# Involutions of a four-layer network: 7x7 as band-matrix products on TensorE, 3x3 summed by identity matmuls

## Chip, cores and metric

One core of a Trainium2 chip runs the whole network. The metric is the device time of one execution in microseconds. Everything is computed in float32.

## What is computed

The input is 16 images of 64 x 64 tokens with 256 channels. Four layers follow each other, each as `x = x + layer(group_norm(x))`: linear attention (layer 0), a gated layer with a selective scan and a batch norm over all images (layer 1), a 3x3 involution (layer 2) and a 7x7 involution (layer 3). The change concerns the end of layer 1 and layers 2 and 3.

```python
def _L2_conv_ref(x, Wr, br, gamma, beta, mean, var, Ws, bs, Wi, bi):
    r = einsum('bhwc,cd->bhwd', x, Wr) + br
    r = relu((r - mean) * rsqrt(var + 1e-3) * gamma + beta)
    w = einsum('bhwd,dk->bhwk', r, Ws) + bs
    w = w.reshape(B, H, W, 16, 9)[:, :, :, :, None, :]
    xi = einsum('bhwc,cf->bhwf', x, Wi) + bi
    patches = stack of the 9 shifted copies of the zero-padded xi
    patches = patches.reshape(B, H, W, 16, 16, 9)
    return sum(w * patches, axis=-1).reshape(B, H, W, 256)

def _L3_conv_ref(x, w_reduce, gamma, beta, mean, var, w_span, b_span):
    r = einsum('bhwc,cd->bhwd', x, w_reduce)
    r = relu((r - mean) * (gamma / sqrt(var + 1e-3)) + beta)
    kgen = (einsum('bhwd,de->bhwe', r, w_span) + b_span).reshape(B, H, W, 16, 49)
    patches = stack of the 49 shifted copies of the zero-padded x
    return einsum('bhwgk,bhwkgc->bhwgc', kgen, patches).reshape(B, H, W, 256)
```

An involution is a convolution whose weights are made at each token from the token itself: 64 reduced features give 9 or 49 weights for each of 16 groups of 16 channels. In layer 2 the patch array is reshaped as it lies in memory: the flat index `q = tap * 256 + channel` is cut into runs of nine, so that an output channel sums nine neighbours of the flat index, which are mostly nine channels of one tap.

## The kernel before

The program has two halves. The first (up to L531) runs layer 0 and most of layer 1 for one image after the other, stores the result channel by channel in the DRAM tile `x1_d`, and collects the statistics of the batch norm. The second half (from L534) runs over the 16 images again. What follows is one image of it.

**End of layer 1 (L613 to L638).** In eight chunks of 512 tokens `x1` is loaded from `x1_d` (L617); the token factors are spread over the partitions by four matmuls (`pf`, L123); ScalarE applies scale and shift (L622), VectorE multiplies by `pf` (L626), ScalarE applies the relu (L627), GpSimd adds `x1` and writes `xl` (L631), VectorE takes the statistics (L637). `xl` holds 128 channels on the partitions and two halves; a token of row 32 g + r, column w lies at (r, w, g), so two rows make a line of 128 tokens.

**Layer 2 projections (L641 to L663).** Each chunk is normalised into `xn` by ScalarE and VectorE (L105, L106). TensorE makes the 64 reduced features (`pr`, L649) and the projection `xi` (`px`, L658). ScalarE writes them to `rt` (L652) and to the padded planes `pad` (L662). GpSimd copies the halo between the two halves (L596, L597).

**3x3 involution (L667 to L710).** Eight groups of four lines. For each of three column shifts TensorE transposes six lines of `pad` (L604) and ScalarE copies them to `xs` (L677), so that 128 tokens lie on the partitions. TensorE makes the weights `pw` in PSUM (L682). VectorE multiplies segment by segment into `pd` (L691, 40 instructions per group, sorted by column shift), sums nine neighbours with one reduction (L698) and adds the residual, which TensorE has transposed into `pres` (L705, L710). The result is `x3`.

**Layer 3 norm and reduction (L713 to L741).** `x3` is transposed back (L718), copied into `pad` (L723), its statistics taken (L727); `pad` is normalised in place (L105, L106), the reduced features are made (L734, L738), and the halo is copied again.

**7x7 involution (L744 to L805).** Four blocks of eight lines; in each, seven column shifts `dj`. Per shift TensorE transposes 14 lines into `xs` (L604, copied out by ScalarE in L756). Per half block of four lines TensorE makes the weights `pk` (L761), VectorE multiplies seven row shifts (L770), GpSimd adds pairs of products (L782), and TensorE sums the four remaining terms in PSUM by multiplying them with the identity (`pacc`, L787). After the seventh shift VectorE adds `x3` (L797) and SyncE stores the rows (L801).

All DMAs are issued on SyncE's queue (SP). The program is written in a framework that puts the instructions of each engine into one order ahead of the run, from data dependences and free buffers; each engine then runs its own list in order and waits on semaphores. Buffers of a pool are reused in turn, and a pool that is closed gives its memory to the next one.

Of the kernel before, what the change touches and what calls it, by code (L numbers as in the profile page):

```python
# [15 lines left out]
P = 128  # L16
# [10 lines left out]
PAD = 3  # L27
PW = HW + 2 * PAD
PR = HW // 2 + 2 * PAD


def involution_segments():
    """The flat patch index q = tap * 256 + channel, cut where the tap, the group (q // 144) or
    a run of nine changes: (tap, first channel, q, groups of nine, elements in each)."""
    cuts = sorted(set(range(0, 2305, 256)) | set(range(0, 2305, 144)))
    out = []
    for a, b in zip(cuts, cuts[1:]):
        head = min(b, -(-a // 9) * 9)
        tail = max(head, b // 9 * 9)
        for lo, hi, n in ((a, head, head - a), (head, tail, 9), (tail, b, b - tail)):  # L40
            if hi > lo:
                out.append((lo // 256, lo % 256, lo, (hi - lo) // n, n))
    # One column shift after the other.
    return sorted(out, key=lambda s: s[0] % 3)
# [3 lines left out]
def network(ctx: ExitStack, tc: tile.TileContext, a: dict, out: bass.AP):  # L48
# [19 lines left out]
    # Kept for all images: gate and normalisation of layer 1 (scale, shift), and its token factor.  # L68
    ab = const("ab", [P, 2, NI, 2])
    fac = const("fac", [P, NI, NB])  # L70
    bnp = const("bnp", [P, 2, 2])
    x1_d = dram.tile([NI, 2, P, NT], F32, tag="x1_d", name="x1_d")

    def inv_sqrt(dst, var, eps):
        """dst = (var + eps) ** -0.5 of a narrow tile"""
        n = dst.shape[-1]
        v = small.tile([P, n], F32, tag=f"isq{n}", name="isq")
        nc.vector.tensor_scalar(v, var, eps, None, ALU.add)  # L78
        nc.gpsimd.tensor_tensor(dst, v, mhalf[:, :n], ALU.pow)  # L79

    def group_norm(stats, pool):
        """Mean and 1/std of each channel's group, [128, 2] each, from its bn_stats."""
# [20 lines left out]
    def normalised(dst, src, gm, rstd, nb):  # L103
        """dst = (src - mean) * rstd over [128, 2, n]: a channel half on each engine."""
# [5 lines left out]
    def affine(dst, src, i):  # L110
        """Layer 1's gated input of image i over [128, 2, n]."""
# [7 lines left out]
    def spread(pf, i, ch):  # L119
        """Token factors of a chunk on every partition."""  # L120
# [10 lines left out]
    # ------------------------------------------------------------------ layers 0 and 1  # L131
    with ExitStack() as st:
# [20 lines left out]
        # Rows of the scan's inputs: delta, delta m m, delta m, m, 1.  # L153
# [10 lines left out]
        # The 7x7 convolution as matrices between the tokens of two row pairs, delta pairs apart.  # L164
# [40 lines left out]
        for i in range(NI):  # L205
            # x, channels on partitions
# [19 lines left out]
            # linear attention, four heads at a time: tokens t = 128 d + p, channels 8 j + head  # L226
            oa = []
            for hf in range(2):
# [32 lines left out]
                # k: softmax over (p, j) for each (d, head); its sum comes with the context  # L261
# [19 lines left out]
                # q: softmax over d for each (p, j, head); its sum divides the product  # L281
# [51 lines left out]
            # output projection, layer norm, residual; statistics for layer 1  # L333
# [57 lines left out]
            # layer 1: channel gate  # L391
# [27 lines left out]
            nc.vector.tensor_scalar(ab[:, 1, i, :], gate, -1.0, None, ALU.mult)  # L419

            # mean and maximum over channels, [p, d] with two zero columns on each side
# [18 lines left out]
            # selective scan: softplus, then the inputs of the recurrence as rows  # L440
# [61 lines left out]
            # statistics of the gated product for the batch norm over all images  # L502
# [13 lines left out]
        # Over images of one size: the mean of their means; of their variances, and the means' own.  # L516
# [21 lines left out]
    # ------------------------------------------------------------------ layers 1 (end), 2, 3  # L538
    with ExitStack() as st:
# [3 lines left out]
        tr = st.enter_context(tc.tile_pool(name="b_tr", bufs=2, space=PSUM))  # L543
# [15 lines left out]
        wsp = bconst("wsp", [65, 7, 112])  # L559
        wspf = wsp.rearrange("p j k -> p (j k)")  # L560
        nc.sync.dma_start(out=wspf[0:64, :], in_=a["w_span"])
        nc.sync.dma_start(out=wspf[64:65, :], in_=a["b_span"])

        def folded(name, mean, var, gamma, beta, shift):
            """(v + shift - mean) * gamma / sqrt(var + eps) + beta as scale and bias, [64, 2]"""
# [6 lines left out]
            sb = bconst(f"{name}_sb", [64, 2])  # L572
# [5 lines left out]
            nc.vector.tensor_tensor(sb[:, 1:2], v[:, 0:1], v[:, 3:4], ALU.add)  # L578
            return sb
# [4 lines left out]
        # From here on a token of row 32 g + r, column w is (r, w, g): two rows are 128 tokens in a  # L584
        # line. The padded planes hold both halves with their halo; what lies outside stays zero.
        pad = big.tile([P, 2, PR, PW, 2], F32, tag="pad", name="pad")
        nc.gpsimd.memset(pad, 0.0)
        # Reduced features, with a row of ones for the bias.
        rt = big.tile([65, NT], F32, tag="rt", name="rt")
        nc.gpsimd.memset(rt[64:65, :], 1.0)  # L590
        lines = pad.rearrange("p c e w g -> p c e (w g)")
        inner = lines[:, :, PAD : PAD + 32, 2 * PAD : 2 * (PAD + HW)]

        def halo():
            cols = pad[:, :, :, PAD : PAD + HW, :]
            nc.gpsimd.tensor_copy(cols[:, :, 0:3, :, 1], cols[:, :, 32:35, :, 0])  # L596
            nc.gpsimd.tensor_copy(cols[:, :, 35:38, :, 0], cols[:, :, 3:6, :, 1])  # L597

        segments = involution_segments()

        def shifted(dst, line, col):
            """The 128 tokens of a line, seen from a shift: dst [128, 256] in PSUM."""
            for h in range(2):
                nc.tensor.transpose(  # L604
                    dst[:, h * P : (h + 1) * P], lines[:, h, line, 2 * col : 2 * col + P], ident
                )

        for i in range(NI):
            xl = big.tile([P, 2, NT], F32, tag="xl", name="xl")
            x3 = big.tile([P, 32, C], F32, tag="x3", name="x3")  # L610
            st0 = wk.tile([P, 2, NCH, 6], F32, tag="st0", name="st0")
            with ExitStack() as ph:
                w1 = ph.enter_context(tc.tile_pool(name="b_w1", bufs=2))  # L613
                for ch in range(NCH):
                    tk = slice(ch * CT, (ch + 1) * CT)
                    x1 = w1.tile([P, 2, CT], F32, tag="x1", name="x1", bufs=3)
                    nc.sync.dma_start(out=x1, in_=x1_d[i, :, :, tk].rearrange("h p t -> p h t"))  # L617
                    pf = sm.tile([P, CT], F32, tag="sm", name="pf")
                    spread(pf, i, ch)
                    for h in range(2):  # L620
                        z = w1.tile([P, CT], F32, tag="z", name="z", bufs=3)
                        nc.scalar.activation(  # L622
                            z, x1[:, h], AF.Identity,
                            bias=ab[:, 1, i, h : h + 1], scale=ab[:, 0, i, h : h + 1],
                        )
                        nc.vector.tensor_tensor(z, z, pf, ALU.mult)  # L626
                        nc.scalar.activation(z, z, AF.Relu, bias=bnp[:, 1, h : h + 1])  # L627
                        dst = xl[:, h].rearrange("p (r w g) -> p g r w", r=32, g=2)[
                            :, ch // 4, ch % 4 * 8 : ch % 4 * 8 + 8, :
                        ]  # L630
                        nc.gpsimd.tensor_tensor(  # L631
                            dst,
                            z.rearrange("p (r w) -> p r w", w=HW),
                            x1[:, h].rearrange("p (r w) -> p r w", w=HW),
                            ALU.add,
                        )
                        nc.vector.bn_stats(st0[:, h, ch, :], dst)  # L637
            _, gm, rstd, nb = group_norm(st0, sm)  # L638

            with ExitStack() as ph:  # L640
                w2 = ph.enter_context(tc.tile_pool(name="b_w2", bufs=2))  # L641
                mm = ph.enter_context(tc.tile_pool(name="b_mm", bufs=2, space=PSUM))
                for ch in range(NCH):
                    tk = slice(ch * CT, (ch + 1) * CT)
                    xn = w2.tile([P, 2, CT], F32, tag="t", name="xn")
                    normalised(xn, xl[:, :, tk], gm, rstd, nb)
                    pr = sm.tile([P, CT], F32, tag="sm", name="pr")
                    for h in range(2):
                        nc.tensor.matmul(  # L649
                            pr[0:64, :], lhsT=wr2[:, h, :], rhs=xn[:, h], start=(h == 0), stop=(h == 1)  # L650
                        )
                    nc.scalar.activation(  # L652
                        rt[0:64, tk], pr[0:64, :], AF.Relu, bias=sb2[:, 1:2], scale=sb2[:, 0:1]
                    )
                    for fh in range(2):
                        px = tr.tile([P, CT], F32, tag="tr", name="px")
                        for h in range(2):
                            nc.tensor.matmul(  # L658
                                px, lhsT=wi[:, h, fh * P : (fh + 1) * P], rhs=xn[:, h],
# [5 lines left out]
                            AF.Identity, bias=bi[:, fh : fh + 1],  # L665
                        )
                halo()  # L667
# [209 lines left out]
```

## Time and profile before

| | us |
|---|---|
| median of 3 runs (21,822.43 to 21,828.05) | 21,826.8 |
| span of the profiled execution | 21,826.7 |
| TensorE matmul busy | 16,690.8 |
| TensorE weight loads busy | 10,255.7 |
| VectorE busy | 14,419.2 |
| GpSimd busy | 7,388.4 |
| ScalarE busy | 5,343.7 |

Busy times are sums over one execution. Weight loads (PEld) run beside matmuls (PE). A line of a table of groups names the source line, the engine and the operation, then output and inputs, the shapes, the number of instructions, the busy time and the mean duration of one, and at the end the idle time of the engine ahead of them with what ended it. In the table by stage each engine has its busy time and, in brackets, its number of instructions; "PEclk" is the granted clock of TensorE as a share of full speed. In a timeline a line has the start, the length and what ran. Matmuls are pipelined: the durations of neighbours overlap, and the cost of one in a row is the distance of two starts.

### The profile page before, as it was taken

Reading aid. Unit: us, or ns where it says so; the run is one execution under the profiler, and the core shown is the slowest. Engines: PE = TensorE matmul, PEld = TensorE weight load, DVE = VectorE, ACT = ScalarE, POOL = GpSimd, SP = SyncE. Lnnn points to the kernel's source line nnn. Section 1 sums busy time; section 2 is a strip of 40 time slices with the busy share of each in tenths; the row PEclk is TensorE's granted clock in tenths of the full one; section 3 lists DMA queues with packets and bytes.
Section 4 is the critical chain, followed back from the end, with each engine's and each line's share of the span. In section 5 each row is a group of like instructions: output and inputs, shape, how many; then the busy total and the mean of one; then the engine's idle time right before and its main releaser. Section 6 shows DMA issues by size and latency. Waiting matters only on the chain.

```text
span 21826.7 us, 175959 instructions
## 1 busy us (share of the span) xinstructions
PE 16690.8 (76%) x66336; PEld 10255.7 (47%) x66336; DVE 14419.2 (66%) x19055; ACT 5343.7 (24%) x8944; POOL 7388.4 (34%) x3593
## 2 busy tenths in 40 slices
PE   6776666666666669779788797797887977878779
PEld 4444444444444434445444454454444544544445
DVE  4444444444444467878778777777787777877878
ACT  2222222222222222222222222222222222222221
POOL 0000110000001016436355363363543634635436
PEclk7777776677777669889889898898987988989889
DMA  0000000000000000000000000000000000000000
GB/s 29 16 16 16 21 19 16 16 24 16 16 18 21 17 6 16 4 12 6 12 14 4 12 16 2 14 6 12 14 4 12 15 3 14 6 10 16 4 12 8
DMA packets 212129, 282.07 MB, mean 13 GB/s; under 512 B 13116, under 2 KB 145421, under 8 KB 211278
## 3 DMA queue, kind: packets, MB, share of 16 engines
q1 hardware_dynamic: 211278, 270.81, 3.7%
q8 instruction: 523, 8.57, 0.2%
q14 instruction: 328, 2.69, 0.0%
HBM read 136.55 MB, written 134.22 MB: 12 GB/s over the span
## 4 chain that ended last, share of the span: by engine, by line
PE 41%; DVE 18%; POOL 4%; issue 3%; ACT 1%; DMA 1%; SPq 0%; DVEq 0%; POOLq 0%; ACTq 0%
PE pacc L787 28%; DVE pd L691 7%; DVE lo L698 6%; PE pt L604 4%; POOL prod L782 3%; PE pk L761 3%; DVE prod L770 2%; PE px L658 2%; PE pr L649 1%; PE pr L734 1%; POOL xl L631 1%; DVE st L727 0%; DVE ot L797 0%; PE pt L718 0%; ACT z L627 0%
## 5 line engine op out<-in xcount | busy, mean ns | idle before, releaser
L770 DVE TENSOR_TENSOR prod<-xs,pk 128x1024 f32<-128x1024 f32 x6272 | 7152.2, 1214 | 1675.0 <-PE pk L761 1405.9
L782 POOL TENSOR_TENSOR prod<-prod 128x1024 f32<-128x1024 f32 x2688 | 6279.3, 2365 | 2612.8 <-DVE prod L770 2594.3
L787 PE MATMUL pacc<-prod,ident 128*128 128x512 f32 x14336 | 6652.3, 598 | 304.5 <-POOL prod L782 304.4
L787 PEld LDWEIGHTS pacc<-prod,ident 128*128 128x128 f32 x14336 | 2528.4, 191 | 2632.0 <-issue 2226.5
L756 ACT COPY xs<-pt 128x512 f32<-128x512 f32 x3136 | 1753.1, 588 | 6852.6 <-PE pt L604 6449.8
L604 PE MATMUL pt<-ident,pad 128*128 128x128 f32 x17152 | 2730.3, 300 | 518.1 <-ACT xs L677 411.9
L604 PEld LDWEIGHTS pt<-ident,pad 128*128 128x128 f32 x17152 | 2183.3, 154 | 1682.3 <-issue 832.9
L691 DVE TENSOR_TENSOR pd<-xs,pw 128x576 f32<-128x576 f32 (+16 forms) x5120 | 1569.5, 386 | 222.2 <-ACT xs L677 222.2
L241 PE MATMUL pq<-wq,xn 128*128 128x384 f32 x4096 | 1398.6, 505 | 135.3 <-DVE va L257 92.3
L79 POOL TENSOR_TENSOR gn_r<-isq,mhalf 128x2 f32<-128x2 f32 x64 | 44.9, 701 | 4227.2 <-DVE isq L78 4227.2
L698 DVE TENSOR_REDUCE lo<-pd 128x1024 f32<-128x9216 f32 x128 | 1247.6, 9747 | 3.3
L761 PEld LDWEIGHTS pk<-wsp,rt 65*128 65x128 f32 x7168 | 959.0, 192 | 417.9 <-issue 417.9
L241 PEld LDWEIGHTS pq<-wq,xn 128*128 128x128 f32 x4096 | 807.5, 198 | 709.2 <-issue 161.4
L677 ACT COPY xs<-pt 128x512 f32<-128x512 f32 x1152 | 634.9, 588 | 1818.0 <-DVE pd L691 1493.3
L761 PE MATMUL pk<-wsp,rt 65*128 65x112 f32 x7168 | 970.2, 272 | 0.0
L286 POOL TENSOR_TENSOR qa<-qa,mq 128x2048 f32<-128x2048 f32 x64 | 231.7, 3642 | 1841.7 <-DVE mq L283 1841.7
L123 PE MATMUL pf<-ident,fac 128*128 128x128 f32 x2048 | 443.1, 388 | 429.4 <-DVE z L626 323.9
L705 PE MATMUL pres<-ident,xl 128*128 128x128 f32 x1024 | 244.9, 408 | 678.4 <-DVE x L710 678.3
L375 PE MATMUL pt<-ident,y 128*128 128x128 f32 x1024 | 268.4, 436 | 638.1 <-DVE y L368 638.1
L423 POOL MEMSET maps<- 128x72 f32 x16 | 2.5, 158 | 1940.1 <-PE psc L491 1940.1
L257 DVE COPY va<-pq 128x256 f32<-128x256 f32 x512 | 215.9, 424 | 661.5 <-ACT ka L253 636.4
L473 DVE TENSOR_TENSOR_SCAN hst<-da,hst,pbc 16x512 f32<-16x512 f32 x112 | 142.0, 1268 | 770.1 <-PE pbc L469 770.1
(186 smaller groups left out, 17910.2 us busy)
## 6 DMA issues: line engine op xcount, KB each, us to landing
xin<-in_x SPq DMA_DIRECT2D x128, 512.0 KB, 4.5
x_d<-xT SPq DMA_DIRECT2D x128, 512.0 KB, 2.8
x<-x_d SPq DMA_DIRECT2D x128, 512.0 KB, 3.6
out<-ot SPq DMA_DIRECT2D x256, 256.0 KB, 2.8
wq<-in_wqkv SPq DMA_DIRECT2D x1, 768.0 KB, 5.0
wo<-in_wout SPq DMA_DIRECT2D x1, 256.0 KB
wi<-in_Wi SPq DMA_DIRECT2D x1, 256.0 KB
bmask<-in_bmask SPq DMA_DIRECT2D x1, 224.0 KB, 2.6
```

Source lines behind the costliest of these rows:

```text
L123: nc.tensor.matmul(pf[:, q * P : (q + 1) * P], lhsT=fac[:, i, d : d + 1].broadcast_to([P, P]), rhs=ident, start=True, stop=True,)
L241: nc.tensor.matmul(pq[:, dd, 0:384], lhsT=xn[:, h, tok], rhs=wq[:, h, hf * 384 : (hf + 1) * 384], start=(h == 0), stop=(h == 1),)
L604: nc.tensor.transpose(dst[:, h * P : (h + 1) * P], lines[:, h, line, 2 * col : 2 * col + P], ident)
L658: nc.tensor.matmul(px, lhsT=wi[:, h, fh * P : (fh + 1) * P], rhs=xn[:, h], start=(h == 0), stop=(h == 1),)
L677: nc.scalar.copy(t[:, e : e + 2, :], pt)
L691: nc.vector.tensor_tensor(pd[:, :, q0 : q0 + n].rearrange("p r (f k) -> p r f k", k=nk), xs[dj][:, di : di + 4, c0 : c0 + n].rearrange("p ...
L698: nc.vector.tensor_reduce(lo, pd.rearrange("p r (o k) -> p r o k", k=9), AX.X, ALU.add)
L756: nc.scalar.copy(xs[:, e : e + 2, :], pt)
L761: nc.tensor.matmul(pk[:, r, 0:112], lhsT=rt[:, row * P : (row + 1) * P], rhs=wsp[:, dj, :], start=True, stop=True,)
L770: nc.vector.tensor_tensor(t.rearrange("p r (g c) -> p r g c", c=16), xs[:, g * 4 + di : g * 4 + di + 4, :].rearrange("p r (g c) -> p r g c ...
L782: nc.gpsimd.tensor_tensor(s, s, t, ALU.add)
L787: nc.tensor.matmul(pacc[:, g * 4 + b * 2 : g * 4 + b * 2 + 2, :], lhsT=ident, rhs=t[:, b * 2 : b * 2 + 2, :], start=(dj == 0 and n == 0), ...
```

## The change

The first half stays; it keeps the group mean of layer 1 besides (`gm1`, one copy of [128, 2] per image). Comments are dropped. In the second half:

- **End of layer 1.** VectorE subtracts the mean and multiplies by the factor in one instruction, ScalarE applies scale, shift and relu in one. `x1` and `z` have two buffers instead of three.
- **Norms folded into weights.** `scaled` multiplies the weights by 1/std per channel and makes the mean's share with small matmuls; `reduced` uses both. The matmuls of layer 2's projections and of both reductions read `xl` and `pad` as they are.
- **3x3 involution.** The products of a group go into two tiles, one per half of the output channels (two buffers); the taps are no longer sorted by column shift. The sum over nine is nine matmuls with the identity per half, over columns of `pd` nine elements apart, and the residual is added in the same PSUM bank by four more. ScalarE copies the result to `x3`. The weights' PSUM tile `pw` has one buffer.
- **Strips.** `x3` is stored to DRAM (`x3_d`), its mean is subtracted in place (three instructions on VectorE, one on GpSimd), and 16 DMAs store it as overlapping strips of 14 columns (`strips`), whose border rows and columns were set to zero once by 36 DMAs.
- **7x7 involution.** The image is cut into 22 x 8 tiles of 3 x 8 tokens; the input patch of a tile is 9 x 14 = 126 tokens. For two ranges of tile rows and two halves of the channels TensorE makes, for each group and each of the 24 output tokens, the 126 weights of that token's patch as a column: the weight matrix `span` is laid out with zeros between its rows of seven, so that a shifted window of 126 of its columns gives a band matrix. The result of all tiles of the range is copied into `wm` (one buffer), by ScalarE and VectorE in turn. Then, tile row by tile row, a patch load `xw` brings 126 tokens on the partitions for eight tiles, and 32 matmuls multiply 32 channels (two groups) by the 48 columns of those two groups' band matrices; of each channel only its own group's 24 columns are kept, by two multiplications with a mask that also holds 1/std (`msk`). Two tile rows are transposed back, the residual `ot`, loaded from `x3_d`, is added, and the rows are stored.

```diff
-            for ch in range(NCH):
-                rows = inner[:, :, ch * 4 : ch * 4 + 4, :]
-                normalised(rows, rows, gm, rstd, nb)
...
-                    lo = w2.tile([P, 4, C], F32, tag="t", name="lo")
-                    nc.vector.tensor_reduce(
-                        lo, pd.rearrange("p r (o k) -> p r o k", k=9), AX.X, ALU.add
-                    )
...
+                    for oh in range(2):
+                        pd = w2.tile([P, 4, P, 9], F32, tag="pd", name="pd")
...
+                        lo = acc.tile([P, 4, P], F32, tag="acc", name="lo")
+                        for k in range(9):
+                            nc.tensor.matmul(
+                                lo, lhsT=ident, rhs=pd[:, :, :, k], start=(k == 0), stop=False
+                            )
+                        for r in range(4):
+                            row = rc * 4 + r
+                            nc.tensor.matmul(
+                                lo[:, r, :], lhsT=xl[:, oh, row * P : (row + 1) * P], rhs=ident,
+                                start=False, stop=(r == 3),
+                            )
+                        nc.scalar.copy(
+                            x3[:, rc * 4 : rc * 4 + 4, oh * P : (oh + 1) * P], lo
+                        )
...
+            for g in range(2):
+                for tj in range(NTC):
+                    lo, hi = max(0, tj * TC - 3), min(HW, tj * TC + TC + 3)
+                    nc.sync.dma_start(
+                        out=strips[
+                            i % 2, tj, 3 + 32 * g : 35 + 32 * g, lo - tj * TC + 3 : hi - tj * TC + 3, :
+                        ].rearrange("r w c -> w r c"),
+                        in_=x3[2 * lo + g : 2 * hi : 2],
+                    )
...
+                for t0, t1 in ((0, 12), (12, NTR)):
+                    nt = (t1 - t0) * NTC
+                    for h in range(2):
+                        wm = []
+                        for q in range(4):
+                            w = w3.tile([P, 2, TILE_OUT, 96], F32, tag=f"wm{q}", name="wm", bufs=1)
+                            wm.append(w)
+                            for n in range(6):
+                                pk = wg.tile([P, 2, 4, P], F32, tag="wg", name="pk")
+                                for m in range(8):
+                                    gg, o = divmod(n * 8 + m, TILE_OUT)
+                                    oi, oj = divmod(o, TC)
+                                    shift = oi * (TC + 6) + oj
+                                    nc.tensor.matmul(
+                                        pk[0:TILE_IN, m // 4, m % 4, 0:nt],
+                                        lhsT=span[
+                                            :, h * 8 + q * 2 + gg, s0 - shift : s0 - shift + TILE_IN
+                                        ],
+                                        rhs=rimg[
+                                            :, oi + TR * t0 : oi + TR * (t1 - 1) + 1 : TR, oj:HW:TC
+                                        ],
+                                        start=True, stop=True,
+                                    )
...
+                                if n % 2:
+                                    nc.vector.tensor_copy(dst, src)
+                                else:
+                                    nc.scalar.copy(dst, src)
+                        for td in range(t0, t1, 2):
...
+                            nc.sync.dma_start(
+                                out=ot[:, 0:nl, :],
+                                in_=x3_d[i % 2, tk, h * P : (h + 1) * P].rearrange(
+                                    "(l p) c -> p l c", p=P
+                                ),
+                            )
                             for k in range(2):
...
+                                xw = w3.tile([P, NTC, P], F32, tag="xw", name="xw", bufs=3)
+                                nc.sync.dma_start(
+                                    out=xw[0:TILE_IN],
+                                    in_=strips[
+                                        i % 2, :, ti * TR : ti * TR + TR + 6, :, h * P : (h + 1) * P
+                                    ].rearrange("t r w c -> (r w) t c"),
                                 )
...
+                                pa = acc.tile([P, 2, TR, HW], F32, tag="ac3", name="pa")
+                                for tj in range(NTC):
+                                    for q in range(4):
+                                        nc.tensor.matmul(
+                                            pa[32 * q : 32 * q + 32].rearrange(
+                                                "c g a w -> c (g a) w"
+                                            )[:, :, tj * TC : (tj + 1) * TC],
+                                            lhsT=xw[0:TILE_IN, tj, 32 * q : 32 * q + 32],
+                                            rhs=wm[q][0:TILE_IN, :, :, (ti - t0) * NTC + tj].rearrange(
+                                                "p g (a w) -> p (g a) w", w=TC
+                                            ),
+                                            start=True, stop=True,
+                                        )
+                                exk = ex[:, k]
+                                pav = pa.rearrange("c g a w -> c g (a w)")
+                                nc.scalar.activation(
+                                    exk, pav[:, 0], AF.Identity, scale=msk[:, h, 0:1]
                                 )
+                                nc.vector.scalar_tensor_tensor(
+                                    exk, pav[:, 1], msk[:, h, 1:2], exk, ALU.mult, ALU.add
+                                )
```

The helpers `scaled` and `reduced`:

```diff
+        def scaled(w, rstd, gm, n, tag):
+            t = wk.tile([P, 2, n], F32, tag=tag, name=tag)
             for h in range(2):
+                nc.vector.tensor_scalar(t[:, h], w[:, h], rstd[:, h : h + 1], None, ALU.mult)
+            pm = sm.tile([P, CT], F32, tag="sm", name="pm")
...
+                    nc.tensor.matmul(
+                        pm[0:m, f : f + 1], lhsT=t[:, h, f * m : (f + 1) * m],
+                        rhs=gm[:, h : h + 1], start=(h == 0), stop=(h == 1),
+                    )
+            return t, pm
+
+        def reduced(w, sb, pm, src, dst, tag):
+            b = small.tile([64, 1], F32, tag=tag, name=tag)
+            nc.vector.tensor_scalar(b, pm[0:64, 0:1], sb[:, 2:3], sb[:, 1:2], ALU.mult, ALU.add)
+            for ch in range(NCH):
+                pr = sm.tile([P, CT], F32, tag="sm", name="pr")
+                for h in range(2):
+                    nc.tensor.matmul(
+                        pr[0:64, :], lhsT=w[:, h, :], rhs=src(h, ch), start=(h == 0), stop=(h == 1)
+                    )
+                for o, v in dst(pr[0:64, :], ch):
+                    nc.scalar.activation(o, v, AF.Relu, bias=b, scale=sb[:, 0:1])
```

## The prediction

> **What bounds the kernel now.** I read the busy table first, then busy time by stage for one image of the second half, then the groups of instructions. The profiled execution spans 21,826.7 us; the median of the runs is 21,826.8, so I sum against the span and add nothing.
>
> ```profile
> PE 16690.8 (76%) x66336; PEld 10255.7 (47%) x66336; DVE 14419.2 (66%) x19055; ACT 5343.7 (24%) x8944; POOL 7388.4 (34%) x3593
> ```
>
> The mean hides stages with different limits. In the table by stage the columns are the stretch, its length, then PE, PEld, DVE, ACT and POOL busy (and instructions), granted clock, DMA share, GB/s:
>
> ```profile
> 0.00:7760.00 7760.00, 5308.66 (x21424) 3625.79 (x21424) 3475.51 (x5956) 1879.75 (x3120) 713.41 (x549) 0.72 0.05 18
> 7760.00:21826.00 14066.00, 11382.10 (x44912) 6629.87 (x44912) 10943.73 (x13100) 3463.95 (x5824) 6674.97 (x3044) 0.88 0.03 10
> 14889.00:15067.00 178.00, 86.73 (x415) 69.64 (x414) 176.55 (x338) 41.54 (x76) 0.00 (x0) 0.61 0.00 0
> 15067.00:15111.00 44.00, 25.99 (x83) 11.68 (x81) 24.26 (x32) 18.22 (x27) 1.00 (x2) 0.74 0.00 1
> 15111.00:15676.00 565.00, 536.90 (x2145) 303.39 (x2144) 456.18 (x400) 110.34 (x197) 393.23 (x170) 0.99 0.02 7
> 15676.00:15716.00 40.00, 13.40 (x52) 11.70 (x52) 22.36 (x40) 23.00 (x32) 21.10 (x17) 0.51 0.37 122
> 15716.00:15766.00 50.00, 47.96 (x116) 17.91 (x117) 4.37 (x10) 23.13 (x33) 1.01 (x2) 0.95 0.00 0
> ```
>
> The first 7,760 us (layers 0 and 1) are left as they are but for one [128,2] copy per image. Sixteen images of 877 us follow: 178 the 3x3 involution (DVE 99% busy), 44 its tail, the norm and the reduction, 565 the 7x7 involution (PE 95% busy at clock 0.99), 40 the end of layer 1, 50 layer 2's projections (PE 96%). The groups say what fills them:
>
> ```profile
> L770 DVE TENSOR_TENSOR prod<-xs,pk 128x1024 f32<-128x1024 f32 x6272 | 7152.2, 1214 | 1675.0 <-PE pk L761 1405.9
> L782 POOL TENSOR_TENSOR prod<-prod 128x1024 f32<-128x1024 f32 x2688 | 6279.3, 2365 | 2612.8 <-DVE prod L770 2594.3
> L787 PE MATMUL pacc<-prod,ident 128*128 128x512 f32 x14336 | 6652.3, 598 | 304.5 <-POOL prod L782 304.4
> L698 DVE TENSOR_REDUCE lo<-pd 128x1024 f32<-128x9216 f32 x128 | 1247.6, 9747 | 3.3
> ```
>
> The code calls L787's matmul 16·4·7·2·4·2 = 7,168 times and the profile has 14,336: a float32 matmul is two passes, each with its own weight load; a transpose (L604, 17,152 calls and records) is one. I price passes from the chain (first line) and the timeline, by start to start, the first three at full clock:
>
> ```profile
> 15185.60 3.45 PE pacc L787 x8
> 15135.18 1.94 PE L761 MATMUL pk<-wsp,rt 65*128 65x112 f32 x16
> 15136.95 1.04 PE L604 MATMUL pt<-ident,pad 128*128 128x128 f32 x8
> 7591.44 0.48 PE L403 MATMUL ph<-av,w1T 128*16 128x2 f32 x4 [1.44 <-DVE av L397]
> ```
>
> So 512 columns take 0.430 us a pass (0.84 ns a column; the load hides); 128 loaded against 112 streamed 0.111 (1.94 less the last one's 0.27 latency, over 15); a transpose 0.114 (the loads of eight take 0.91).
>
> **7x7 involution, 565 us an image.** All of L604, L756, L761, L770, L782 and L787 goes here. Added on PE: (a) the bands, 2 row ranges · 2 halves · 4 · 6 · 8 = 768 calls = 1,536 passes of 126 loaded, 96 or 80 streamed: L761's 0.111 each, 170.5 us. (b) the products, 44 tiles · 8 · 4 = 1,408 calls = 2,816 passes of 32 loaded and 48 streamed. Nothing so narrow is in the trace. From below 48·0.84+3 = 43 ns; from above L604's 114. L403 (16 loaded, 2 streamed) does four passes in 0.48 us, of which 0.17 is the last one's latency and one gap a semaphore wait; the two passes of one call start 49 ns apart. I take 55, near that row: 155 us; by the ends 121 and 321. (c) 64 transposes, 7 us. With 10 us for the turns between the four blocks: 342 us.
>
> [...]
>
> What must hide beside that: evacuating the bands, 96 copies of 768 or 640 elements, ACT 0.80 us (588 ns for 512, 0.83 ns an element more), DVE 0.95 (1,220 for 1,024 and 672 for 512 from PSUM), one of each per 3.55 us of PE. Per tile one ACT and one DVE instruction of 192 elements and half an add of 384, under 0.8 us each against 3.7 of PE. Uncovered, the copies would be 84 us an image. DMA: a tile's patch load is 1,008 packets of 512 B, and half an `ot` load and half a store add 384. All packets before took 3.7% of 16 engines, 61 ns each at a mean of 1,282 B; by bytes 24 ns, so 2.1 us a tile, and 5.3 if as dear as the mean packet: then +1.6 us a tile, 70 us an image. I take the first (close to bytes: `x` lands in 3.6 us with 256 packets, `xin` in 4.5 with 512). SP issues 106 transfers more per image; at 0.66 (four `out` issues in 2.64 us) 70 us, beside everything.
>
> **3x3 involution, 178 us.** DVE loses L698 (9.75) and L710 (1.22) of its 23.3 us per group of rows and keeps products of 12.3. PE per group now: 36 passes of 512 over `pd` (9 per half, two halves, two passes), 15.5; residual 16 passes 1.8; 36 transposes 4.1; `pw` 8 passes 1.25: 22.65 us, where it had 10.8 busy. So PE bounds it, and nearly all of DVE's gain is taken back. In-order, the next group's transposes and `pw` (one buffer now) wait for DVE's last product and then for what PE has queued: if both sums go ahead of them 27.6, so 25: 200 us, +18 for fill and tail that the 178 and the 44 share. The taps are no longer sorted by column shift, so the first products need all three shifts: 3 us once an image, in the 18. The ACT copies out of PSUM (2·0.59) lie under it.
>
> **The rest.** Reduction and projections no longer wait for normalised copies: 32 + 64 passes of 0.43 are 41 us, with group norm and the small scaled-weight matmuls 48 instead of 50. End of layer 1: ACT loses one of two passes, but `x1` and `z` go from three buffers to two; a load of 3.6 plus 4.4 of use over two buffers is 4.2 a chunk where it was 3.4: 44 us for 40 (35 if ACT was all). Norm and reduction of layer 3: 20.5. Storing `x3` (4 MB, some 13 us), subtracting means (three DVE and one POOL instruction of 2,048: 2.3 and 3.6), then 16 strip stores (6.8 MB, 25 to 40 us) end about 45 to 60 us after the norm, and the first patch load waits for all of them; the reduction and the first block of bands (14 + 43 us) cover this. Without the cover it costs 40 us an image. Once: 36 zero stores, 24 us.
>
> **Sum per image:** 44 + 48 + 200 + 18 + 20.5 + 342 + 4 (end) = 676.5 against 877: -200.5, times 16 = -3,208, +24. Forecast **18,640 us**.
>
> **Rival 1, slower: PE reading scattered columns.** All three new moving operands step over memory: `pd` 36 B, `rimg` 32 B, `wm` 384 B; every moving operand of before is contiguous. On DVE this costs: L263 reads 4,096 elements 512 B apart in 7,174 ns, 1.716 a piece after the 147 of fixed cost, where L698 needs 1.04; L637 and L384, 8 B apart and contiguous, both take 694. If PE pays DVE's 1.716 ns a column instead of 0.84: 3x3 331 + 18, bands 1,536 passes of 168 or 140 ns = 236.5, products 2,816·0.0854 = 240; period 959, total **23,140**. It decides from 1.52 ns a column up, where the period is 877 again. For it: DVE's rows. [...]
>
> [...]
>
> **Rival 2: narrow passes are not cheap.** (b) at 114 ns: +166 us an image, 21,300. For it: the loads of 32 columns change column groups each time. **Rival 3: the patch load is exposed once per pair.** SP is in order; if a pair's store (which waits for the last add) stands ahead of the next loads, each of 22 pairs waits some 5.4 us (3.6, 4.5 and one halving of packets more): +119, 20,500. Three buffers of `xw` speak against it.
>
> **Numbers.** Chances: forecast 0.46 (its own range 17,600 to 20,200: passes from 43 to 90 ns, the 3x3 from 22.65 us a group, the end of layer 1 from 35, DMA to its dear end), rival 1 0.38 (0.35 of it slower, 0.02 even, 0.01 faster), rival 2 0.09, rival 3 0.07 (0.01 slower, with part of rival 1). Within 0.2% cannot be told from no change. Faster 0.62, same 0.02, slower 0.36. The range reaches to 23,500, past rival 1's price; what is beyond both ends is about 0.15.
>
> **What would show it.** Forecast right: L787's successor over `pd` at 0.43 a pass, band passes near 0.111, product passes under 0.07, DVE far below half busy, the 7x7 stage near 340 us. Rival 1: the passes over `pd` near 0.88 and band passes above 0.14 at full clock. Rival 2: product passes at 0.11 with 32-column loads back to back. Rival 3: PE waiting for `xw` in every pair. The forecast also falls if the 3x3 stage is well above 220 us because PE and DVE take turns.

## The result, and the profile after

After: 22,736.0 us median of four runs (22,728.9 to 22,741.9), before 21,827.4 beside it; ratio 1.0417, 95% interval 1.0402 to 1.0431. The change makes the kernel 909 us slower; 18,640 was forecast. The profiled execution spans 22,740.0 us.

The busy table of after: DVE went from 14,419 us to 7,009, POOL from 7,388 to 1,184, as meant. PE rose by 2,232 and now sets the end.

```profile
PE 18923.2 (83%) x108896; PEld 12933.3 (57%) x108896; DVE 7008.9 (31%) x14258; ACT 4268.8 (19%) x7152; POOL 1183.9 (5%) x889
```

The table by stage of one image of after (columns as in the table of before): end of layer 1, projections, 3x3, tail with norm and reduction, 7x7.

```profile
20864.00:20905.00 41.00, 14.03 (x58) 12.16 (x58) 22.95 (x39) 12.91 (x16) 20.17 (x16) 0.54 0.34 106
20905.00:20953.00 48.00, 46.50 (x118) 19.91 (x118) 1.67 (x9) 17.24 (x24) 0.71 (x1) 0.93 0.00 0
20953.00:21307.00 354.00, 324.73 (x773) 116.41 (x772) 99.54 (x322) 48.25 (x89) 0.55 (x2) 0.96 0.00 0
21307.00:21347.00 40.00, 31.84 (x101) 15.71 (x98) 23.61 (x34) 15.91 (x30) 7.16 (x2) 0.70 0.40 129
21347.00:21800.00 453.00, 438.09 (x4424) 420.20 (x4424) 72.86 (x114) 54.97 (x94) 0.00 (x0) 0.65 0.30 83
```

The 7x7 stage fell from 565 us to 453, the 3x3 stage rose from 178 to 354: 936 us an image where it was 877 and should have been 676.5. Both large stages are full of PE, but one runs at clock 0.96 and the other at 0.65. The groups of after:

```profile
L845 PE MATMUL pk<-rt,span 65*126 65x96 f32 (+1 forms) x24576 | 5180.7, 395 | 45.0 <-ACT wm L862 34.5
L753 PE MATMUL lo<-pd,ident 128*128 128x512 f32 x4608 | 4250.5, 1091 | 396.3 <-DVE pd L743 396.3
L743 DVE TENSOR_TENSOR pd<-xs,pw 128x576 f32<-128x576 f32 (+16 forms) x5120 | 1573.2, 385 | 4082.0 <-ACT xs L725 4082.0
L886 PE MATMUL pa<-wm,xw 126*32 126x48 f32 x45056 | 1650.0, 323 | 67.0 <-DMA xw<-strips 42.4
```

Busy time over count prices a pass (the mean of one overlaps its neighbours): a band pass (L845) 0.211 us where 0.111 was taken, a pass over `pd` (L753) 0.92 for 0.43, a product pass (L886) 0.037 for 0.055. In these two stages PE waits little for others: 396 us for `pd` and 42 for `xw` over all 16 images. Two lines of the timeline of after (start, length, line, count, idle before) show the same shape of 512 columns twice:

```profile
20924.56 27.71 PE L699 MATMUL px<-xl,wis 128*128 128x512 f32 x64
21272.11 16.73 PE L753 MATMUL lo<-pd,ident 128*128 128x512 f32 x18 [5.45 <-DVE pd L743]
```

Contiguous, 64 passes take 27.71 us, 0.43 each; stepping 36 bytes, 18 take 16.73, 0.93. From start to start the records of L753 give 0.910 us in the median at full clock and also at 0.5: this price does not follow the clock.

### The profile page after: what moved, and what is told of

Read it like the earlier page. It is cut to its first block, busy times and chain, and to the rows that moved or that the text cites. A ratio compares the mean times of both kernels' runs of the same rounds, so it can differ in the third digit from the quotient of the medians.

```text
span 22740.0 us, 250346 instructions
## 1 busy us (share of the span) xinstructions
PE 18923.2 (83%) x108896; PEld 12933.3 (57%) x108896; DVE 7008.9 (31%) x14258; ACT 4268.8 (19%) x7152; POOL 1183.9 (5%) x889
## 5 line engine op out<-in xcount | busy, mean ns | idle before, releaser
L845 PE MATMUL pk<-rt,span 65*126 65x96 f32 (+1 forms) x24576 | 5180.7, 395 | 45.0 <-ACT wm L862 34.5
L845 PEld LDWEIGHTS pk<-rt,span 65*126 65x126 f32 x24576 | 5132.7, 326 | 86.1 <-ACT wm L862 46.9
L753 PE MATMUL lo<-pd,ident 128*128 128x512 f32 x4608 | 4250.5, 1091 | 396.3 <-DVE pd L743 396.3
L753 PEld LDWEIGHTS lo<-pd,ident 128*128 128x128 f32 x4608 | 981.5, 218 | 3251.6 <-issue 2824.9
L860 DVE COPY wm<-pk 126x768 f32<-126x768 f32 (+1 forms) x768 | 684.3, 891 | 4333.9 <-PE pk L845 4232.7
L886 PE MATMUL pa<-wm,xw 126*32 126x48 f32 x45056 | 1650.0, 323 | 67.0 <-DMA xw<-strips 42.4
L886 PEld LDWEIGHTS pa<-wm,xw 126*32 126x32 f32 x45056 | 1449.1, 146 | 204.1 <-issue 130.5
L725 ACT COPY xs<-pt 128x512 f32<-128x512 f32 x1152 | 625.5, 590 | 934.5 <-DVE pd L743 780.7
L721 PE MATMUL pt<-ident,pad 128*128 128x128 f32 x4608 | 645.6, 281 | 72.5 <-ACT xs L725 64.1
L721 PEld LDWEIGHTS pt<-ident,pad 128*128 128x128 f32 x4608 | 499.9, 141 | 189.5 <-ACT xs L725 160.6
```

Source lines behind the costliest of these rows:

```text
L721: nc.tensor.transpose(pt[:, k, h * P : (h + 1) * P], lines[:, h, rc * 4 + e + k, 2 * j : 2 * j + P], ident,)
L725: nc.scalar.copy(t[:, e : e + 2, :], pt)
L753: nc.tensor.matmul(lo, lhsT=ident, rhs=pd[:, :, :, k], start=(k == 0), stop=False)
L845: nc.tensor.matmul(pk[0:TILE_IN, m // 4, m % 4, 0:nt], lhsT=span[:, h * 8 + q * 2 + gg, s0 - shift : s0 - shift + TILE_IN], rhs=rimg[:, oi ...
L860: nc.vector.tensor_copy(dst, src)
L886: nc.tensor.matmul(pa[32 * q : 32 * q + 32].rearrange("c g a w -> c (g a) w")[:, :, tj * TC : (tj + 1) * TC], lhsT=xw[0:TILE_IN, tj, 32 * ...
```

## The experiments

Three questions were open: is it the stride that makes `pd` dear, what halves the clock in the bands, and why are the products cheap. Results with an interval come from four executions, the others from one, which is enough for the steps of hundreds of us looked at here.

**1. `pd` in planes.** One plane of 128 columns per neighbour:

```diff
-pd = w2.tile([P, 4, P, 9], F32, tag="pd", name="pd")
+pd = w2.tile([P, 4, 9, P], F32, tag="pd", name="pd")
...
-lo, lhsT=ident, rhs=pd[:, :, :, k], start=(k == 0), stop=False
+lo, lhsT=ident, rhs=pd[:, :, k, :], start=(k == 0), stop=False
```

> Only pd is stored another way: nine planes of 128 columns per row in place of nine neighbours, so the nine-fold sum's moving operand is runs of 128 contiguous columns; DVE now writes with a stride. Theory (PE pays for the 36-byte stride, 0.91 us a pass by the trace of after): passes over pd fall to 0.43 us as in the projections, 36 passes of a group fall from 33 to 15.5 us, and the 3x3 stage from 354 to about 205 us (PE 22.65 us a group, or DVE's 12.3 us of products and their wait), so about -2.3 ms: 20,400 us. Rival (an accumulating identity matmul of this shape is 0.91 us whatever the layout, or DVE's strided writes cost what PE gains): no change in the passes, 22,700 us; if only DVE's writes cost more (1.7 ns an element, 31 us a group in place of 12.3), PE passes fall to 0.43 but DVE bounds the stage at some 250 to 300 us: about 21,500 us.

20,954.7 us (expected 20,400), ratio to before 0.9603 (0.9588 to 0.9617): 1,781 us less than after. The groups of this run:

```profile
L752 PE MATMUL lo<-pd,ident 128*128 128x512 f32 x4608 | 2222.4, 640 | 671.9 <-DVE pd L742 671.9
L742 DVE TENSOR_TENSOR pd<-xs,pw 128x576 f32<-128x576 f32 (+16 forms) x5120 | 2152.9, 545 | 2038.0 <-ACT xs L725 2038.0
```

PE's busy time on the sum falls by 2,028 us: 0.429 us a pass from start to start, the contiguous price. The theory holds for the passes. 276 us of the gain come back as waits for `pd` (396 before, 672 now): DVE's products now write with a stride, 16.8 us a group of rows in place of 12.3 (L742 over 128 groups), and PE and DVE take turns. The stage falls to about 243 us, not 205.

**2. The price by stride.** The nine matmuls of a half read with steps of 1 to 9 elements, so this kernel no longer sums the nine neighbours; only its pass prices are of use (22,095.5 us in all):

```diff
-for k in range(9):
-    nc.tensor.matmul(lo, lhsT=ident, rhs=pd[:, :, :, k], start=(k == 0), stop=False)
+nc.tensor.matmul(lo, lhsT=ident, rhs=pdf[:, :, 0 : 128 : 1], start=True, stop=False)
+nc.tensor.matmul(lo, lhsT=ident, rhs=pdf[:, :, 0 : 256 : 2], start=False, stop=False)
...
+nc.tensor.matmul(lo, lhsT=ident, rhs=pdf[:, :, 0 : 1152 : 9], start=False, stop=False)
```

> The nine identity matmuls of each half read pd with strides of 1, 2, 3 ... 9 elements, one stride each, on a line of its own; what is summed is therefore not the nine neighbours, and the output is another. Theory (a fixed price per fetch of 16 bytes: two elements at 8 bytes still come together, from 16 bytes on each element pays alone): 0.43 us a pass at 1 and 2 elements, 0.9 us from 4 on, 3 between. Rival A (price grows with the stride): a steady rise up to 0.91 at 9. Rival B (any stride costs the same): 0.43 at 1 and 0.91 from 2 on. Rival C (the passes are long for another reason): all alike at 0.91.

The groups of this run for steps of 1, 2, 3, 4 and 9 elements (each busy time holds also some 0.1 us a pass of overlap with the next line, and the passes that met half clock):

```profile
L752 PE MATMUL lo<-pd,ident 128*128 128x512 f32 x512 | 273.7, 616 | 3.5 <-DVE pd L743 0.4
L753 PE MATMUL lo<-pd,ident 128*128 128x512 f32 x512 | 334.2, 738 | 315.7 <-DVE pd L743 315.7
L754 PE MATMUL lo<-pd,ident 128*128 128x512 f32 x512 | 420.4, 911 | 0.0
L755 PE MATMUL lo<-pd,ident 128*128 128x512 f32 x512 | 505.1, 1076 | 0.0
L760 PE MATMUL lo<-pd,ident 128*128 128x512 f32 x512 | 512.5, 1090 | 0.0
```

Start to start at full clock, median: 0.432, 0.451, 0.666, 0.899 us for 1 to 4 elements, then 0.895 to 0.919 up to 9. That is close to 1.76 ns for each 16 bytes touched (steps of 2, 3 and 4 touch 256, 384 and 512 such pieces: 451, 676 and 901 ns). With a step of 1 all four elements of a piece are used, 128 pieces would be 225 ns, and PE's 0.84 ns a column (0.432 us measured for 512) is the larger. This is a price that fits the nine steps; what makes it is not shown. The theory's numbers came; the rivals' (a rise to 9, one price for any step) did not.

**3. The image sorted for the bands.** The reduced image is kept with a tile's columns together:

```diff
-rimg = rt.rearrange("k (r w) -> k r w", w=HW)
+rimg = rt.rearrange("k (r o t) -> k r o t", o=TC, t=NTC)
...
-:, oi + TR * t0 : oi + TR * (t1 - 1) + 1 : TR, oj:HW:TC
+:, oi + TR * t0 : oi + TR * (t1 - 1) + 1 : TR, oj, :
```

> Only the reduced image is stored another way (columns sorted by their place within the 8-column tile), so that the bands' moving operand is runs of 16 contiguous columns in place of single elements 32 bytes apart. T1 (the strided read starves PE, and the granted clock of 0.5 follows from that): band passes fall from 0.213 to about 0.111 us, clock near 1.0 in those stretches, 1,536 passes an image give about -150 us an image, -2.4 ms: 20,300 us. T2 (the clock is granted at half for another reason, such as 65 of 128 rows in use): clock stays 0.5, passes stay at about 0.21 us, the load of 126 columns at half clock, and the time stays within 1% of 22,740 us.

22,539.8 us, ratio to before 1.0327 (1.0310 to 1.0345): only 196 us less than after. Windows inside a block of bands, first of after, then of this run:

```profile
21352.00:21430.00 78.00, 78.00 (x369) 78.00 (x367) 11.49 (x12) 8.79 (x11) 0.00 (x0) 0.50 0.35 90
```

```profile
21186.00:21256.00 70.00, 70.00 (x330) 70.00 (x330) 9.88 (x11) 7.98 (x10) 0.00 (x0) 0.50 0.32 82
```

PE is busy without a gap, at half clock, in both; one pass in 0.211 and 0.212 us. Of the 24,576 band passes 88% still run at half clock at 0.213 us from start to start, and the others took 0.110 where after's took 0.147 (80 columns) and 0.175 (96). T2 holds: the starved read is not what halves the clock; it was hidden beneath it.

**4. and 5. 128 rows in the bands**, on the sorted image and on after. The 63 rows added to `span` are zeros, so the sum is the same:

```diff
-span = bconst("span", [65, 16, SPAN], a["span"].rearrange("k (g s) -> k g s", g=16))
+span = bconst("span", [P, 16, SPAN])
+nc.gpsimd.memset(span, 0.0)
+nc.sync.dma_start(out=span[0:65], in_=a["span"].rearrange("k (g s) -> k g s", g=16))
...
-rt = big.tile([65, (HW + 2) * HW], F32, tag="rt", name="rt")
+rt = big.tile([P, (HW + 2) * HW], F32, tag="rt", name="rt")
```

> The image sorted by columns as in the run with that alone (22,540 us), and the bands' contraction widened from 65 to 128 rows: the 63 more rows of the span matrices are zeros, those of the image ones, so that the sum is the same. T_rows (the chip grants half the clock because only 65 of 128 rows work): granted clock near 1.0 in the stretches of bands, 0.110 us a pass in place of 0.213, some 21,700 passes at half clock times 103 ns = -2.2 ms: 20,300 us. T_other (it follows from the many short passes with a load each, or from what values the rows carry): clock stays 0.5 and the time 22,540 us.

> Only the bands' contraction widened to 128 rows (63 of zero weights), the image left with its columns 32 bytes apart. With the clock at 1.0 the strided read shows: 16-byte pieces at 1.76 ns each, 96 columns in 0.172 us and 80 in 0.146 (after's few passes at full clock: 0.175 and 0.147): 24,576 passes at 0.159 us in place of 0.211, -1.3 ms: 21,450 us, 1.15 ms above the run with 128 rows and sorted image. Rival (the starved reads keep the clock at half even with 128 rows): 22,740 us.

20,298.8 us with the sorted image (expected 20,300), 21,660.8 without it (expected 21,450). The band groups, first with the sorted image, then with after's:

```profile
L847 PE MATMUL pk<-rt,span 128*126 128x80 f32 x12288 | 1387.5, 273 | 20.2 <-ACT wm L864 20.2
L847 PE MATMUL pk<-rt,span 128*126 128x96 f32 x12288 | 1361.5, 273 | 29.0 <-ACT wm L864 14.6 <-ACT rt L650 14.3
```

```profile
L847 PE MATMUL pk<-rt,span 128*126 128x96 f32 x12288 | 2167.1, 355 | 24.9 <-ACT wm L864 14.5 <-ACT rt L650 10.4
L847 PE MATMUL pk<-rt,span 128*126 128x80 f32 x12288 | 1935.1, 335 | 20.3 <-ACT wm L864 20.3
```

0.112 us a pass in the first, 0.167 in the second, where the strided read shows (0.175 us for 96 columns from start to start; 6% of the passes still met half clock, part of the 210 us over the expectation). A window inside the bands of the run with the sorted image has the clock:

```profile
18662.00:18698.00 36.00, 36.00 (x330) 36.00 (x329) 8.44 (x11) 7.55 (x11) 0.00 (x0) 1.00 0.08 22
```

As many passes (330) as took 70.00 us in run 3 take 36.00 here. Each of these two runs has 64 unbroken stretches of 340 band passes or more, and all begin at full clock. With 65 rows at work all 64 end at half clock, with 128 all 64 end at full clock, though 63 of the rows multiply by zero. T_rows holds for this pair. Not separated is whether the number of rows counts or that the added ones carry data (ones in the image), and no number between 65 and 128 was run. The two faults hide one another:

| bands | image as in after | image sorted |
|---|---|---|
| 65 rows | 22,736 us | 22,540 us |
| 128 rows | 21,661 us | 20,299 us |

Sorting is worth 196 us at half clock and 1,362 at full.

**6. One column group at a time.** The products' loops turned:

```diff
-for tj in range(NTC):
-    for q in range(4):
+for q in range(4):
+    for tj in range(NTC):
```

> Only the order of the products' two inner loops is turned: eight tiles of columns in one 32-column group after the other, where after steps through the four column groups each time. Theory (passes in different column groups run side by side, so 48 strided columns at 1.78 ns = 85 ns appear as 37 ns): with one group at a time the pass is about 85 ns, 45,056 passes +48 ns = +2.2 ms: about 24,900 us. Rival (narrow passes are simply cheap and follow each other): no change, 37 ns a pass and 22,740 us.

24,100.8 us. The product group of this run:

```profile
L886 PE MATMUL pa<-wm,xw 126*32 126x48 f32 x45056 | 3146.6, 261 | 0.0
```

70 ns a pass where after's order took 37, with the same instructions: passes in different column groups overlap. The size was less than expected (+1.36 ms, not +2.2). From start to start the median is 83 ns, near the 84 that 48 pieces at 1.76 come to; a fifth of the passes start less than 30 ns after the one before and pull the mean down. What lets these through stays open.

**7. to 9. The band matrices by tile**, so that the products read contiguously: `wm` as `[P, 96, 2 * TILE_OUT]` and `rhs=wm[q][0:TILE_IN, (ti - t0) * NTC + tj, :]`; alone, with 1 and 3, and with 128 rows as well.

> Only the band matrices are stored another way (one row of 48 weights per tile, so that the products' moving operand is contiguous; the copies out of PSUM write single elements 192 bytes apart). After takes 37 ns a product pass with four column groups in turn, and 70 ns with one group at a time. Theory A (the strided reads bound the passes, side by side or not): the pass falls to 15 to 25 ns, -0.5 to -1.0 ms: 21,750 to 22,250 us. Theory B (the pace of issue or of the weight loads bounds them): 37 ns stays, 22,740 us. Theory C (the scattered writes of ACT and DVE cost more than the reads save): PE waits for wm, slower than 22,740 us.

> All three moving operands contiguous: pd in planes, the image sorted by column in the tile, wm by tile; otherwise as after. The gains add if the three stages are apart: planes of pd -1,781 us and the sorted image -196 us (both as measured alone), the band matrices 0 to -1,000 us: 19,750 to 20,760 us. Rival (they share a limit, such as the clock): less than the sum of the parts, above 20,800 us.

> Three contiguous operands and 128 rows in the bands. If T_rows holds: the time of the run with three contiguous operands less some 2.2 ms, 17,600 to 18,600 us, near the forecast of 18,640 us and under the kernel before. If not: that run's own time, 19,750 to 20,760 us.

The product group of the run with `wm` by tile alone, and the two band groups of the run with all four:

```profile
L884 PE MATMUL pa<-wm,xw 126*32 126x48 f32 x45056 | 1051.5, 259 | 365.0 <-DMA xw<-strips 258.1 <-issue 80.6 <-DVE wm L858 15.0
```

```profile
L846 PE MATMUL pk<-rt,span 128*126 128x80 f32 x12288 | 2368.1, 386 | 38.6 <-ACT wm L861 35.4 <-issue 3.2
L846 PE MATMUL pk<-rt,span 128*126 128x96 f32 x12288 | 1411.5, 278 | 38.9 <-ACT wm L861 24.5 <-ACT rt L650 14.3
```

Alone 22,570.1 us, only 166 less than after: the pass falls to 23 ns, as theory A had it, but the waits for `xw` grow from 42 to 258 us and 71% of the product passes run at half clock, where 14% of after's did. All three layouts: 20,773.7 (expected 19,750 to 20,760), ratio 0.9519 (0.9503 to 0.9535), all but no gain over planes and sorted image (1,781 + 196 would give 20,759). With 128 rows: 19,360.3, ratio 0.8872 (0.8859 to 0.8885), where 17,600 to 18,600 was expected: the 96-column bands run at full clock, the 80-column ones mostly do not. Two stretches of 340 passes of 80-column bands of one image in this last run, and a window inside each:

```profile
19182.26 72.66 PE L846 MATMUL pk<-rt,span 128*126 128x80 f32 x340
19286.34 37.52 PE L846 MATMUL pk<-rt,span 128*126 128x80 f32 x340
```

```profile
19184.00:19254.00 70.00, 70.00 (x330) 70.00 (x330) 12.31 (x10) 12.81 (x11) 0.00 (x0) 0.50 0.03 9
19287.00:19323.00 36.00, 36.00 (x330) 36.00 (x329) 12.39 (x10) 13.21 (x11) 0.00 (x0) 1.00 0.09 25
```

The same work takes 72.66 us at clock 0.50 or 37.52 at 1.00. Which it gets goes with the clock at its start: of the 32 such stretches in the trace 26 begin at half clock and stay there to their end, and 6 begin at full clock and keep it. Stretches of 96 columns recover: the 16 that begin at half clock are at full clock within 1.2 to 4.0 us. So in this run 128 rows did not bring the clock back for the 80-column passes that began at half clock (none of 26 stretches). Ahead of them run the products, 55% of whose passes are at half clock here. In run 10 below, which differs by `wm` alone (kept as in after), 1% are, and all 32 stretches begin and end at full clock. Why the contiguous products are granted less stays open.

**10. to 12. Without `wm` by tile, and with the old 3x3 sum.** Run 10 is planes, sorted image and 128 rows. The other two take the 3x3 sum back to DVE (on after, and with sorted image and 128 rows):

```diff
-for k in range(9):
-    nc.tensor.matmul(lo, lhsT=ident, rhs=pd[:, :, :, k], start=(k == 0), stop=False)
+lo = x3[:, rc * 4 : rc * 4 + 4, oh * P : (oh + 1) * P]
+nc.vector.tensor_reduce(lo, pd, AX.X, ALU.add)
...
+nc.vector.tensor_tensor(lo, lo, res, ALU.add)
```

> pd in planes, image sorted by column in the tile, 128 rows in the bands; the band matrices as in after. The sorted image with 128 rows measured 20,299 us, planes save 1,781 us: 18,520 us, below the 19,360 us of the run that also has the band matrices by tile, because the products then run at full clock and the bands after them too. Rival (planes and the clock interact): the bands fall to half clock in some stretches, 19,000 us or more.

> Only the 3x3 part of the change is undone: DVE adds the nine neighbours again (one reduction of 9.75 us per half and group of rows where after has 18 passes over pd) and adds the residual, which PE transposes. The 3x3 stage goes back from 354 us an image to the 178 to 190 us of before: -164 to -176 us an image, 19,920 to 20,120 us, faster than before; the 7x7 part by itself is then the gain. Rival (what the 3x3 loses comes partly from its neighbours, such as the xs buffers or the order of the segments): above 20,500 us.

> The 3x3 part undone (DVE adds the nine neighbours and the residual), with the sorted image and 128 rows in the bands. If the stages are apart: 20,299 us less 164 to 176 us an image, 17,480 to 17,680 us. Rival (the longer idle of PE in the 3x3 stage leaves the clock low in the 7x7 stage): above 18,000 us.

Run 10: 18,537.4 us (expected 18,520), ratio 0.8494 (0.8480 to 0.8508). Old 3x3 sum on after: 20,117.8 (expected 19,920 to 20,120), faster than before. Old 3x3 sum with sorted image and 128 rows: 17,710.6 (expected 17,480 to 17,680), ratio 0.8116 (0.8104 to 0.8128), the fastest of all. The 3x3 gave back 162 to 164 us an image, at or just under the low end of what was expected. The table by stage of run 10 (3x3, tail, 7x7):

```profile
17284.00:17528.00 244.00, 197.73 (x774) 112.89 (x774) 135.63 (x322) 48.62 (x90) 0.01 (x1) 0.90 0.00 1
17528.00:17566.00 38.00, 27.73 (x101) 12.81 (x99) 23.13 (x34) 19.23 (x31) 7.17 (x2) 0.87 0.43 140
17566.00:17864.00 298.00, 284.53 (x4422) 267.46 (x4421) 73.18 (x114) 54.13 (x93) 0.00 (x0) 1.00 0.45 126
```

The parts close: planes 1,781 plus sorting and rows 2,437 are 4,218 us; run 10 is 4,199 below after.

## Why the prediction was wrong

Per image, forecast against after, in us:

| term | forecast | after |
|---|---|---|
| end of layer 1, projections | 44 + 48 | 41 + 48 |
| 3x3 with fill and tail, norm, reduction | 200 + 18 + 20.5 | 354 + 40 |
| bands (L845 / 16) | 170.5 | 323.8 |
| products (L886 / 16) | 155 | 103.1 |
| rest of the 7x7 stage | 21 | 26 |
| sum | 676.5 | 936 |

(The forecast's terms add up to 677; the prediction rounds the 7x7 stage down to 342.)

**Two steps failed.** The first is "36 passes of 512 over `pd` [...], 15.5" us a group: they take 32.8. The prediction saw the stride and had two prices at hand, PE's own 0.84 ns a column from contiguous reads and DVE's 1.716 from L263. The forecast took the first, rival 1 the second; that the first holds for a stepped read was the author's estimate, and no row of before shows it. Experiments 1 and 2 decide against it: 0.910 us a pass with steps of 36 bytes, 0.429 in planes, and about 1.76 ns for each 16 bytes touched, so one element of them per column takes twice PE's own 0.84 ns, very near DVE's 1.716.

The second is (a), the bands at "L761's 0.111 each, 170.5 us". Neither the forecast nor any rival had what happened: 0.211 us because the clock is granted at 0.5, with PE busy for 78.00 of 78.00 us in the window of experiment 3. L761 had 65 rows as well, but stood in short runs among L787's full passes, in a stage at clock 0.99; its price was carried over without that company (that the full passes beside it kept its clock up is an inference; no run tests it). Experiments 3 to 5 separate stride and rows. With both mended, the bands of run 10 cost 171.8 us an image (1,387.6 + 1,361.5 over 16): the term itself was right for full clock.

**What held.** The 7x7 stage left DVE and POOL as described; copies, strips and patch loads stay hidden (PE's waits for `xw` before L886 are 42 us in all), so rival 3 falls. Rival 2 falls too: product passes take 37 ns, not 114, and even less than the 55 taken, because they overlap across column groups (experiment 6: 70 ns with one group at a time). The 25 us a group for the 3x3 is not met by any run: with passes at 0.43 the stage takes 244 us, 30.5 a group, with PE and DVE taking turns. But there DVE's strided writes cost 4.5 us a group more than the forecast had, and how much of the 5.5 comes from them and how much from the turns is not separated. In run 10 this and the cheap products cancel (3x3 with tail 282 for 238.5, 7x7 298 for 346): its 18,537 us agrees with the forecast of 18,640 in sum better than in its parts.

**Rival 1** had the sign, and the right mechanism in the 3x3 stage: with tail, norm and reduction 369.5 us against 394 measured. Its total, 23,140 against 22,736, is near partly by chance: its bands (168 and 140 ns) were too cheap for want of the clock, and its products (85 ns) too dear for want of the overlap.

Three sums of the prediction are off by little, and none decides anything. Rival 1's 959 us an image give 23,160 with the 24 us paid once. A load of 3.6 plus 4.4 us over two buffers is 4.0 a chunk, not 4.2. The 106 more transfers count 16 row stores that were there before.

## What to carry to other kernels

Price a moving operand of PE by the 16-byte pieces it touches (1.76 ns each in experiment 2), and lay the tile out so that the inner step is contiguous; check what that does to the engine that writes it (DVE here: 16.8 us a group in place of 12.3). A contiguous pass's price holds only for the clock it was measured at (512 columns: 0.43 us at 1.0, 0.85 at 0.5): before carrying it to a long stretch of its own, ask how many rows of the array work there, and if few, try padding with zero rows (here 64 of 64 stretches ended at half clock with 65 rows and 64 of 64 at full clock with 128). Look also at the clock with which the stretch begins (in the run with all four, the 80-column stretches kept theirs in 32 of 32). Where two limits cover one another (half clock and starved reads here), mending one alone shows little (sorting 196 us, sorting and rows 2,437): test the pair.

## What was not expected

- A PE without a gap was held at clock 0.50 through some 70 us at a time with 65 rows at work; zero rows up to 128 brought 1.00 and 2,241 us (22,540 to 20,299).
- The strided pass (L753 of after) costs 0.910 us at clock 1.0 and at 0.5; a contiguous one (L787 of before) 0.43 and 0.85.
- With the products' operand contiguous, the 80-column bands with 128 rows kept the clock they began with, half or full, in 32 of 32 stretches of 340 passes.
- The order of two inner loops is worth 1,365 us: 37 against 70 ns a pass.
- Making the products' operand contiguous lost time where the rest was mended: 19,360 against 18,537 us, with the 80-column bands at 2,368.1 us busy instead of 1,387.6.
- After's 3x3 sum on PE is slower than DVE's even with its operand contiguous: 18,537 against 17,711 us with the same 7x7 stage.
